# Recurrence of an LSTM layer: the matmul blocks of a step reordered and cut, the output gate apart, and the sums of outputs by accumulating DMAs

## The chip, the cores and the metric

The kernel runs on one core of a Trainium2 chip. The metric is device time in microseconds (us) for the whole kernel, the median of several runs. A second number, the span, comes from one profiled execution: it reaches from the first to the last instruction that the profiler recorded.

The engines are PE (TensorE; PEld is its weight load), DVE (VectorE), ACT (ScalarE), POOL (GpSimd) and SP (SyncE, which here only issues DMAs). SBUF is the on-chip memory of 128 partitions, PSUM the memory that PE writes to.

## The reference

Two layers over x of shape 32 x 512 x 256. The first is graph attention and a Mamba block, the second graph attention and an LSTM. The LSTM runs over the 512 positions of each of the 32 sequences, with hidden size 256, one position after the other. What matters here is this last part (names as in the reference):

```
def step(carry, xp):
    h, c = carry
    gates = xp + h @ W_hh.T
    i, f, g, o = jnp.split(gates, 4, axis=-1)
    c = jax.nn.sigmoid(f) * c + jax.nn.sigmoid(i) * jnp.tanh(g)
    h = jax.nn.sigmoid(o) * jnp.tanh(c)
    return ((h, c), h)
...
logits = jnp.einsum('bth,lh->btl', lstm_out, W_lin) + b_lin
g = jax.lax.stop_gradient(jnp.argmax(logits, axis=-1).astype(lstm_out.dtype))[..., None]
w = g * lstm_out
inc = jnp.cumsum(w, axis=1)
prefix = inc - w
suffix = inc[:, -1:, :] - inc
return 2.0 * lstm_out + prefix * fw_att + suffix * bw_att
```

The result is added to the layer's input x. With two logits, the argmax is a comparison of a difference with a level.

## The kernel before

**Up to 2541 us** the graph and Mamba layers run (`layers_per_batch`). Among this work, POOL also prepares the LSTM's weights in DRAM (`recurrence_weights`): gates in another order, halves folded in, and the rows fw and bw scaled by 0.5. The layers' result lies in DRAM as X3.

**The recurrence** (`recurrence`, one step per t, 512 steps in 32 chunks of CH = 16). The state of 32 sequences times 256 hidden units is laid out on 128 partitions as 4 quarters (Q) of 32 sequences, with J = 64 hidden units each along the free axis. These 64 are two halves of H = 32. Every step does:

- PE multiplies h by the weights `whh`. h is in two tiles, h[0] and h[1], one for each half (called h0 and h1 below). The gate columns of a quarter, 258, are in two PSUM banks: pg0 with 96 columns (the gates f, i, g of half 0, three times 32), and pg1 with 162 (the same gates of half 1, 96; o of both halves, 64; and two columns for the logits). `part` issues four blocks, h0 for pg0, h0 for pg1, h1 for pg0, h1 for pg1, of four matmuls each, one per quarter, side by side in the array. A float32 matmul shows as two records. All of them add to what `x_part` has put in the banks one step ahead: the input's share of the gates, 16 more matmuls for the next step, behind the four blocks in PE's queue.
- ACT takes tanh of pg0 (L1472), then of 160 columns of pg1 (L1473, half 1's gates and o together). A sigmoid is made of a tanh with the halves folded into the weights.
- DVE computes for each half ab (L1478) and the new cell state z (L1481); ACT takes tanh of it (L1483); DVE computes hh (L1491) and transposes it into h0 or h1 (L1495) for the next step.
- DVE then selects by the logits (g, L1502), does one item of the list `extra`, and adds g to the running sum pp (L1508). At the first step of a chunk it also copies the last pp into the new tile (L1510).

PE, DVE and ACT execute in the order in which the code is written (a manual schedule); SP and POOL are ordered by the framework's scheduler, each in its own queue.

`extra` holds the work of the chunk before and after: four `stats` (bn_stats of the next inputs, L1336; the fourth also has POOL compute rstd, L132 and L134), four `norms` taken two per step (L1342; each with a POOL memset), and ten items of `results`. `turning` says at which steps of the chunk PE transposes a normalised input tile: 5, 6, 10, 11.

`results` makes the outputs of the previous chunk on DVE, in two halves of 8 positions: x3 (the residual, loaded by SP from X3 at L1364) plus hh (L1378), plus pp times fw (L1381, L1384), minus pp times bw (L1387, L1390), each on 128 x 512. SP then stores x3 into R, a tile in SBUF that gathers all outputs (L1399).

**The end.** What is still missing is the total times bw. `tot` (L1513) is spread by 16 small DMAs from SP, ACT and POOL into `tots` (L1518); the results of the last chunk are made; then 17 DVE operations add `tots` to R (L1526), and each is followed by four stores to `out`, two on SP and two on ACT (L1528).

Of the kernel before, what the change touches and what calls it, by code (L numbers as in the profile page):

```python
# [9 lines left out]
F32 = mybir.dt.float32  # L10
# [3 lines left out]
AF = mybir.ActivationFunctionType  # L14
ALU = mybir.AluOpType
# [4 lines left out]
P = 128  # L20
N = 512
NT = N // P
D = 256
DK = D // P
# [9 lines left out]
GB = 32  # L34
CH = 16
# [1144 lines left out]
def recurrence_weights(nc, pool, a, wr, now):  # L1180
# [8 lines left out]
    Q, J = 4, 64  # L1189
    W = 4 * J + 2  # L1190
# [3 lines left out]
    order = (3, 1, 0, 2)  # L1194
# [30 lines left out]
    for l in range(2):  # L1225
        for q in range(Q):
            nc.gpsimd.dma_start(
                out=wl[q * 32 : (q + 1) * 32, l * DK : (l + 1) * DK],
                in_=a.wl[q : q + 1, l * J : (l + 1) * J].rearrange("o (k p) -> p (o k)", p=32),
# [12 lines left out]
    t, _ = ordered(b[0], Q, 1, 1.0)  # L1242
# [6 lines left out]
    for n, src in enumerate((a.fw, a.bw)):  # L1249
        for q in range(Q):  # L1250
            nc.gpsimd.dma_start(out=t[q * GB : (q + 1) * GB, n * J : (n + 1) * J], in_=src[q : q + 1, :].to_broadcast([GB, J]))
        yield
    nc.gpsimd.tensor_scalar(t[:, : 2 * J], t[:, : 2 * J], 0.5, None, ALU.mult)
    yield
    nc.gpsimd.dma_start(out=wr[:, n0 : n0 + 2 * J], in_=t[:, : 2 * J])
    yield
# [33 lines left out]
def recurrence(ctx, tc, c, a, X3, wr, out):  # L1290
# [25 lines left out]

    TQ = T // 4
    R = wp.tile([P, TQ, D], F32, name="R")


    NX = CH // 4
# [35 lines left out]

        return tuple([lambda f=f, n=n: f(n) for n in range(NX)] for f in (stats, norm, turn))

    def results(t0, hh, pp):  # L1360

        x3 = ch.tile([P, CH, J], F32, tag="x3", name=f"x3_{t0}")
        for q in range(Q):
            nc.sync.dma_start(  # L1364
                out=x3[q * GB : (q + 1) * GB],
                in_=X3[t0 : t0 + CH, :, q * J : (q + 1) * J].rearrange("t b j -> b t j"),
            )
        todo = []
        n = CH // 2
        for s in (slice(0, n), slice(n, CH)):  # L1370
            r = x3[:, s, :]
            pf = pp[:, s.start : s.stop, :]
            pb = pp[:, s.start + 1 : s.stop + 1, :]
            m = st.tile([P, n, J], F32, tag="m", bufs=1, name=f"m{t0}_{s.start}")
            bc = [P, n, J]

            def one_(r=r, s=s):
                nc.vector.tensor_tensor(r, r, hh[:, s, :], ALU.add)  # L1378

            def two_(m=m, pf=pf):  # L1380
                nc.vector.tensor_tensor(m, pf, fw.unsqueeze(1).to_broadcast(bc), ALU.mult)  # L1381

            def three(r=r, m=m):
                nc.vector.tensor_tensor(r, r, m, ALU.add)  # L1384

            def four(m=m, pb=pb):
                nc.vector.tensor_tensor(m, pb, bw.unsqueeze(1).to_broadcast(bc), ALU.mult)  # L1387

            def five(r=r, m=m):
                nc.vector.tensor_tensor(r, r, m, ALU.subtract)  # L1390

            todo += [one_, two_, three, four, five]
        last_ = todo.pop()

        def gathered():
            last_()
            tq, r0 = t0 // TQ, t0 % TQ
            for q in range(Q):
                nc.sync.dma_start(  # L1399
                    out=R[tq * GB : (tq + 1) * GB, r0 : r0 + CH, q * J : (q + 1) * J], in_=x3[q * GB : (q + 1) * GB]  # L1400
                )

        return todo + [gathered]


    PARTS = ((0, 3 * H), (3 * H, W))

    def part(pg, w, lhs, order, start, stop):

        for k, n in order:  # L1410
            p, (s, e) = pg[n], PARTS[n]
            for q in range(Q):
                nc.tensor.matmul(  # L1413
                    p[q * GB : (q + 1) * GB, :], lhs[k], w[:, k, q, s:e],
                    start=(start and k == 0), stop=(stop and k == DK - 1),
                )

    def x_part(t, xT):

        pg = [psg.tile([P, e - s], F32, tag=f"pg{n}", name=f"pg{n}_{t}") for n, (s, e) in enumerate(PARTS)]  # L1420
        r = (t % G) * GB
        part(pg, wih, [xT[t % CH // G][:, k, r : r + GB] for k in range(DK)], ((0, 0), (1, 0), (0, 1), (1, 1)), True, t == 0)
        return pg

    with tc.manual_schedule(engines={mybir.EngineType.PE, mybir.EngineType.DVE, mybir.EngineType.Activation}):
# [18 lines left out]
        for t in range(T + 1):  # L1444
            s = t % CH
            last = t == T
            if s == 0 and not last:
                t0 = t
                hh_was, pp_was = hh, pp
                hh = ch.tile([P, CH, J], F32, tag="hh", name=f"hh{t0}")  # L1450
                if t:
                    pp = ch.tile([P, CH + 1, J], F32, tag="pp", name=f"pp{t0}")
                assert not extra and not turning
                xT, nxt = nxt, [None] * 2
                stats, norms, turns = normalised(t0 + CH, nxt) if t0 + CH < T else ([], [], [])
                more = results(t0 - CH, hh_was, pp_was) if t else []
                both = [lambda fs=norms[n : n + 2]: [f() for f in fs] for n in range(0, len(norms), 2)]
                extra = stats + both + more
                turning = {(5, 6, 10, 11)[n]: f for n, f in enumerate(turns)}
            if last:  # L1460

                pg = [None, psg.tile([P, W - 3 * H], F32, tag="pg1", name="pglast")]
                part(pg, whh, h, ((0, 1), (1, 1)), True, True)
            elif t:
                part(pg, whh, h, ((0, 0), (0, 1), (1, 0), (1, 1)), False, True)
            pgs = pg
            if not last:
                if t + 1 < T:
                    pg = x_part(t + 1, xT if t + 1 < t0 + CH else nxt)
                turned = [turning.pop(s)()] if s in turning else []  # L1470

                nc.scalar.activation(z[:, H : 4 * H], pgs[0], AF.Tanh)  # L1472
                nc.scalar.activation(z[:, 5 * H : 10 * H], pgs[1][:, : 5 * H], AF.Tanh)  # L1473
                z2 = st.tile([P, 12 * H + 1], F32, tag="z", name=f"z{t + 1}")
                for n in range(2):
                    c0 = 4 * n * H
                    ab = st.tile([P, 2 * H], F32, tag=f"ab{n}", name=f"ab{n}_{t}")
                    nc.vector.scalar_tensor_tensor(  # L1478
                        ab, z[:, c0 + 2 * H : c0 + 4 * H], 1.0, z[:, c0 : c0 + 2 * H], ALU.add, ALU.mult
                    )  # L1480
                    nc.vector.scalar_tensor_tensor(z2[:, c0 : c0 + H], ab[:, :H], 0.5, ab[:, H:], ALU.mult, ALU.add)  # L1481
                for n in range(2):
                    nc.scalar.activation(z[:, (10 + n) * H : (11 + n) * H], z2[:, 4 * n * H : (4 * n + 1) * H], AF.Tanh, scale=0.5)  # L1483

                nc.scalar.copy(z2[:, 12 * H :], level)
                for f in turned:
                    f()
                h = []
                for n in range(2):
                    half = hh[:, s, n * H : (n + 1) * H]  # L1490
                    nc.vector.scalar_tensor_tensor(  # L1491
                        half, z[:, (8 + n) * H : (9 + n) * H], 1.0, z[:, (10 + n) * H : (11 + n) * H], ALU.add, ALU.mult
                    )
                    h.append(st.tile([P, GB], F32, tag=f"h{n}", name=f"h{n}_{t}"))
                    nc.vector.transpose(h[n], half)  # L1495
                z = z2
            if t:

                i = (t - 1) % CH
                p_, h_ = (pp_was, hh_was) if s == 0 and not last else (pp, hh)  # L1500
                g_ = st.tile([P, J], F32, tag="g", name=f"g{t}")
                nc.vector.scalar_tensor_tensor(  # L1502
                    g_, pgs[1][:, 5 * H : 5 * H + 1].to_broadcast([P, J]), level, h_[:, i, :], ALU.is_gt, ALU.mult,
                )
            if extra and not last:
                extra.pop(0)()
            if t:
                nc.vector.tensor_tensor(p_[:, i + 1, :], p_[:, i, :], g_, ALU.add)  # L1508
                if s == 0 and not last:
                    nc.vector.tensor_copy(pp[:, 0, :], p_[:, CH, :])  # L1510
# [1 line left out]
        tot = wp.tile([P, J], F32, name="tot")  # L1512
        nc.vector.tensor_tensor(tot, pp[:, CH, :], bw, ALU.mult)  # L1513

        tots = wp.tile([P, D], F32, name="tots")
        for n in range(4 * Q):
            tq, q = n // Q, n % Q
            (nc.sync, nc.scalar, nc.gpsimd)[n % 3].dma_start(  # L1518
                out=tots[tq * GB : (tq + 1) * GB, q * J : (q + 1) * J], in_=tot[q * GB : (q + 1) * GB]
            )  # L1520
        for f in results(T - CH, hh, pp):
            f()
        t0 = 0
        for step in [2, 6] + [8] * (TQ // 8 - 1):
            r = R[:, t0 : t0 + step, :]
            nc.vector.tensor_tensor(r, r, tots.unsqueeze(1).to_broadcast([P, step, D]), ALU.add)  # L1526
            for tq in range(4):
                (nc.sync, nc.scalar)[tq % 2].dma_start(  # L1528
                    out=out[:, tq * TQ + t0 : tq * TQ + t0 + step, :], in_=r[tq * GB : (tq + 1) * GB]
                )  # L1530
            t0 += step


PERIOD, PIECES = 100234, 49
# [121 lines left out]
```

## Time and profile before

| | us |
|---|---|
| median of 3 runs | 3853.72 (3853.17 to 3853.76) |
| the profiled execution's own time | 3853.91 |
| its span | 3852.2 |

Busy time in the span: PE 3417.8 us (89%), DVE 3256.5 (85%), ACT 2403.0 (62%), POOL 1510.6 (39%). The mean granted TensorE clock is 0.975 of full speed.

How to read the rows. A row of the timeline has the start in us from the span's start, the length, the engine, the line of the kernel, the operation, output<-inputs by the kernel's names, the shapes, the number of instructions merged into the row, and in brackets the idle time of the engine before it with what ended it. A row of the waits has the waiting engine and line, what it waited for, the total in us, the number of times and the longest. A row of the windows has the stretch, its length, busy us and number of instructions of PE, PEld, DVE, ACT and POOL, then the granted clock, the share of the 16 DMA engines and GB/s. A row of the groups has line, engine, operation, shapes and count, then busy us and the mean ns of one, then the idle time before and what ended it. A matmul's end is modelled, and matmuls overlap, so the starts are what is compared.

### The profile page before, as it was taken

The numbers are of one execution on the slowest core, as the hardware profiler recorded it, in microseconds if no ns is written. First come the engines' busy times: TensorE is split into PE (matmuls) and PEld (weight loads), VectorE is DVE, ScalarE is ACT, GpSimd is POOL, SyncE is SP. The second block draws the span as 40 slices with busy tenths as digits, with TensorE's granted clock in tenths as the row PEclk, the third lists the DMA queues.
The fourth block names the chain that finished last, engine by engine and source line by source line (L and its number), as shares of the span: only waits on it lengthen the run. The fifth ranks groups of instructions, "written<-read, shape, count | busy, mean of one in ns | idle before, by whom it ended". The sixth has DMA issues, their size and how long they took to land. (4 is left out here: it accounts for less than half of the span.)

```text
span 3852.2 us, 117182 instructions
## 1 busy us (share of the span) xinstructions
PE 3417.8 (89%) x47370; PEld 2313.5 (60%) x47370; DVE 3256.5 (85%) x10671; ACT 2403.0 (62%) x6434; POOL 1510.6 (39%) x1581
## 2 busy tenths in 40 slices
PE   5999999999999999999999998668888888888882
PEld 3466566556656656655665664446666666666661
DVE  3888888888888888888888886459999999999997
ACT  2777777777777777777777775435454544444441
POOL 3456556555555655655555566710000000000000
PEclk8999999999999999999999998789999999999996
DMA  3322322222223232232223212221222222222226
GB/s 98 89 91 73 101 85 75 94 86 86 83 93 90 72 102 86 72 95 86 86 83 96 87 61 59 82 66 41 44 46 43 46 43 46 43 46 43 46 40 191
DMA packets 271800, 288.76 MB, mean 75 GB/s; under 512 B 151589, under 2 KB 221953, under 8 KB 269073
## 3 DMA queue, kind: packets, MB, share of 16 engines
q1 hardware_dynamic: 265248, 266.96, 25.0%
q10 hardware_dynamic: 3152, 8.76, 0.7%
q8 instruction: 375, 6.14, 0.7%
q0 software_dynamic: 2848, 5.45, 0.5%
q14 instruction: 177, 1.44, 0.1%
HBM read 227.09 MB, written 37.11 MB: 69 GB/s over the span
## 5 line engine op out<-in xcount | busy, mean ns | idle before, releaser
L1413 PE MATMUL pg<-wall,h 128*32 128x96 f32 x16352 | 559.0, 277 | 176.8 <-DVE h L1495 169.4
L1413 PEld LDWEIGHTS pg<-wall,h 128*32 128x32 f32 x16352 | 374.4, 109 | 350.8 <-DVE h L1495 331.9
L1413 PE MATMUL pg<-wall,xTr 128*32 128x96 f32 (+1 forms) x16384 | 549.0, 274 | 0.0
L1413 PEld LDWEIGHTS pg<-wall,xTr 128*32 128x32 f32 x16384 | 447.2, 110 | 5.2 <-issue 0.3
L132 POOL TENSOR_SCALAR ve<-mv 128x4 f32<-128x4 f32 x32 | 6.3, 195 | 1038.5 <-DVE mv L1337 1038.5
L1472 ACT ACTIVATE z<-pg 128x96 f32<-128x96 f32 x512 | 128.7, 251 | 438.9 <-PE pg L1413 438.9
L102 DVE SCALAR_TENSOR_TENSOR w<-rb,colsa,adjT 128x512 f32<-128x512 f32 x512 | 380.4, 778 | 6.0 <-DMA rb<-linea 6.0
L102 DVE SCALAR_TENSOR_TENSOR acc<-px,convw,acc 128x511 f32<-128x511 f32 (+2 forms) x480 | 335.3, 735 | 7.6 <-ACT acc L102 6.4
L1483 ACT ACTIVATE z<-z 128x32 f32<-128x32 f32 x1024 | 234.7, 229 | 168.5 <-DVE z L1481 100.9
L102 ACT ACTIVATE g<-bc,cs 128x128 f32<-128x128 f32 x1024 | 326.0, 399 | 13.1 <-PE py L102 13.1
L102 PE MATMUL px<-mT,win 128*128 128x512 f32 x640 | 307.2, 603 | 0.0
L102 PE MATMUL po<-wc,xh 128*128 128x256 f32 x1024 | 254.3, 392 | 13.5 <-POOL xh L102 8.4
L102 POOL TENSOR_SCALAR ve<-bnmv 128x4 f32<-128x4 f32 x96 | 18.8, 196 | 626.3 <-DVE bnmv L102 607.7
L102 PE MATMUL pav<-w,hb 128*64 128x512 f32 x1024 | 250.1, 608 | 8.0 <-DVE w L102 8.0
L102 PE MATMUL pov<-wb,wv 128*128 128x257 f32 x1024 | 250.5, 392 | 7.0 <-DVE wv L102 5.8
L1495 DVE STREAM_TRANSPOSE h<-hh 128x32 f32<-128x32 f32 x1024 | 216.4, 211 | 34.8
L102 PE MATMUL pz<-mT,win 128*128 128x512 f32 x512 | 245.4, 602 | 0.0
L102 POOL TENSOR_TENSOR rs<-ve,mhalf 128x4 f32<-128x4 f32 (+1 forms) x192 | 237.8, 1239 | 13.3
L1478 DVE SCALAR_TENSOR_TENSOR ab<-z 128x64 f32<-128x64 f32 x1024 | 226.0, 221 | 15.3 <-ACT z L1472 12.0
L102 PEld LDWEIGHTS po<-wc,xh 128*128 128x128 f32 x1024 | 189.5, 193 | 76.6 <-issue 27.0
L1481 DVE SCALAR_TENSOR_TENSOR z<-ab 128x32 f32<-128x32 f32 x1024 | 196.9, 192 | 35.1
L102 POOL TENSOR_SCALAR msk<-adj 128x1024 bf16<-128x1024 int32 x64 | 218.8, 3434 | 13.0 <-DMA adj<-in_adj_dram 7.9
(258 smaller groups left out, 7987.8 us busy)
## 6 DMA issues: line engine op xcount, KB each, us to landing
bc<-line SPq DMA_DIRECT2D x128, 512.0 KB
adj<-in_adj_dram SPq DMA_DIRECT2D x32, 1024.0 KB
rb<-linea SPq DMA_DIRECT2D x64, 512.0 KB
ce<-line SPq DMA_DIRECT2D x64, 384.0 KB
x<-in_x_dram SPq DMA_DIRECT2D x32, 512.0 KB
X<-x SPq DMA_DIRECT2D x32, 512.0 KB
xt<-X SPq DMA_DIRECT2D x128, 128.0 KB
x<-X SPq DMA_DIRECT2D x128, 128.0 KB
```

The source lines that it names most:

```text
L102: return getattr(getattr(self.nc, engine), op)(*map(real, a), **{n: real(v) for n, v in k.items()})
L132: nc.gpsimd.tensor_scalar(ve, var, scale, eps, ALU.mult, ALU.add)
L1413: nc.tensor.matmul(p[q * GB : (q + 1) * GB, :], lhs[k], w[:, k, q, s:e], start=(start and k == 0), stop=(stop and k == DK - 1),)
L1472: nc.scalar.activation(z[:, H : 4 * H], pgs[0], AF.Tanh)
L1478: nc.vector.scalar_tensor_tensor(ab, z[:, c0 + 2 * H : c0 + 4 * H], 1.0, z[:, c0 : c0 + 2 * H], ALU.add, ALU.mult)
L1481: nc.vector.scalar_tensor_tensor(z2[:, c0 : c0 + H], ab[:, :H], 0.5, ab[:, H:], ALU.mult, ALU.add)
L1483: nc.scalar.activation(z[:, (10 + n) * H : (11 + n) * H], z2[:, 4 * n * H : (4 * n + 1) * H], AF.Tanh, scale=0.5)
L1495: nc.vector.transpose(h[n], half)
```

## The change

Four edits.

- The order of the blocks in PE's queue: h0 for pg0; h0 for the columns 0 to 110 of pg1; h1 for pg0; h0 for the columns 110 to 162 of pg1; h1 for pg1.
- ACT's second tanh is split into 96 columns (half 1's gates) and 64 (o).
- The outputs of a chunk are summed by three accumulating DMAs from POOL (hh, pp times fw, pp times bw, added to x3 in SBUF); DVE only makes the products, eight of 128 x 256 in place of ten operations of 128 x 512. bw is negated in the weights for that. The norms are taken one per step, and the order of the extras and the steps of `turning` change: four stats, one product, four norms, seven products; turns at 6, 7, 10, 11.
- At the end, the total is spread over the partitions by four matmuls with a selection matrix `sel` (made by four POOL copies) into PSUM and subtracted from R there; the products of the last chunk come behind the second and third of these operations, and its stores to R are issued by POOL.

```diff
-    nc.gpsimd.tensor_scalar(t[:, : 2 * J], t[:, : 2 * J], 0.5, None, ALU.mult)
+    for n, scale in enumerate((0.5, -0.5)):
+        nc.gpsimd.tensor_scalar(t[:, n * J : (n + 1) * J], t[:, n * J : (n + 1) * J], scale, None, ALU.mult)
...
+        nc.gpsimd.dma_start(out=x3, in_=hh, accum_op=ALU.add)
         todo = []
...
+        for n, w in enumerate((fw, bw)):
+            m = ch.tile([P, CH, J], F32, tag=f"m{n}", bufs=1, name=f"m{n}_{t0}")
+            for s in range(0, CH, 4):
+
+                def product(n=n, w=w, m=m, s=s):
+                    nc.vector.tensor_tensor(
+                        m[:, s : s + 4, :], pp[:, s + n : s + n + 4, :], w.unsqueeze(1).to_broadcast([P, 4, J]), ALU.mult
+                    )
+                    if s + 4 == CH:
+                        nc.gpsimd.dma_start(out=x3, in_=m, accum_op=ALU.add)
+
+                todo.append(product)
...
+    CUT = 110
+    WHOLE = tuple((k, n, 0, W) for n in range(2) for k in range(DK))
+    LATER = ((0, 0, 0, W), (0, 1, 0, CUT), (1, 0, 0, W), (0, 1, CUT, W), (1, 1, 0, W))
...
-                part(pg, whh, h, ((0, 0), (0, 1), (1, 0), (1, 1)), False, True)
+                part(pg, whh, h, LATER, False, True)
...
-                both = [lambda fs=norms[n : n + 2]: [f() for f in fs] for n in range(0, len(norms), 2)]
-                extra = stats + both + more
-                turning = {(5, 6, 10, 11)[n]: f for n, f in enumerate(turns)}
+                extra = stats + more[:1] + norms + more[1:] if t else stats + norms
+                turning = {(6, 7, 10, 11)[n]: f for n, f in enumerate(turns)}
...
-                nc.scalar.activation(z[:, H : 4 * H], pgs[0], AF.Tanh)
-                nc.scalar.activation(z[:, 5 * H : 10 * H], pgs[1][:, : 5 * H], AF.Tanh)
+                for n in range(2):
+                    nc.scalar.activation(z[:, (4 * n + 1) * H : (4 * n + 4) * H], pgs[n][:, : 3 * H], AF.Tanh)
+                nc.scalar.activation(z[:, 8 * H : 10 * H], pgs[1][:, 3 * H : 5 * H], AF.Tanh)
...
+            if T // 2 <= t < T // 2 + Q:
+                q = t - T // 2
+                nc.gpsimd.tensor_copy(
+                    sel[:, q, :].rearrange("p (t b) -> p t b", b=GB),
+                    c.ident[:, q * GB : (q + 1) * GB].unsqueeze(1).to_broadcast([P, 4, GB]),
+                )
...
-        for f in results(T - CH, hh, pp):
-            f()
+        tots = psx.tile([P, DK, P], F32, tag="px", name="tots").rearrange("p k e -> p (k e)")
+        for q in range(Q):
+            nc.tensor.matmul(
+                tots[:, q * J : (q + 1) * J],
+                sel[:, q, :], tot,
+                start=True, stop=True,
+            )
+        rest = results(T - CH, hh, pp, nc.gpsimd)
...
-            nc.vector.tensor_tensor(r, r, tots.unsqueeze(1).to_broadcast([P, step, D]), ALU.add)
+            nc.vector.tensor_tensor(r, r, tots.unsqueeze(1).to_broadcast([P, step, D]), ALU.subtract)
...
+            if n:
+                for f in rest[:4]:
+                    f()
+                rest = rest[4:]
```

More of the change, by code (lines that the diff above doesn't have):

```diff
@@ L1318, in recurrence @@
     R = wp.tile([P, TQ, D], F32, name="R")
+    sel = wp.tile([P, Q, P], F32, name="sel")
     NX = CH // 4
@@ L1358, in normalised, with results @@
         return tuple([lambda f=f, n=n: f(n) for n in range(NX)] for f in (stats, norm, turn))
-    def results(t0, hh, pp):
+    def results(t0, hh, pp, queue=nc.sync):
         x3 = ch.tile([P, CH, J], F32, tag="x3", name=f"x3_{t0}")
@@ L1367, in results @@
             )
+        nc.gpsimd.dma_start(out=x3, in_=hh, accum_op=ALU.add)
         todo = []
[L1369 to L1392, printed above, removed]
+        for n, w in enumerate((fw, bw)):
[8 more added lines that the diff above has]
+                todo.append(product)
         last_ = todo.pop()
@@ L1398, in gathered @@
             for q in range(Q):
-                nc.sync.dma_start(
+                queue.dma_start(
                     out=R[tq * GB : (tq + 1) * GB, r0 : r0 + CH, q * J : (q + 1) * J], in_=x3[q * GB : (q + 1) * GB]
@@ L1406, in recurrence @@
     PARTS = ((0, 3 * H), (3 * H, W))
+    CUT = 110
+    WHOLE = tuple((k, n, 0, W) for n in range(2) for k in range(DK))
+    LATER = ((0, 0, 0, W), (0, 1, 0, CUT), (1, 0, 0, W), (0, 1, CUT, W), (1, 1, 0, W))
     def part(pg, w, lhs, order, start, stop):
-        for k, n in order:
+        for k, n, c0, c1 in order:
             p, (s, e) = pg[n], PARTS[n]
+            s, e = s + c0, min(s + c1, e)
             for q in range(Q):
                 nc.tensor.matmul(
-                    p[q * GB : (q + 1) * GB, :], lhs[k], w[:, k, q, s:e],
+                    p[q * GB : (q + 1) * GB, s - PARTS[n][0] : e - PARTS[n][0]], lhs[k], w[:, k, q, s:e],
                     start=(start and k == 0), stop=(stop and k == DK - 1),
@@ L1421, in x_part @@
         r = (t % G) * GB
-        part(pg, wih, [xT[t % CH // G][:, k, r : r + GB] for k in range(DK)], ((0, 0), (1, 0), (0, 1), (1, 1)), True, t == 0)
+        part(pg, wih, [xT[t % CH // G][:, k, r : r + GB] for k in range(DK)], WHOLE, True, t == 0)
         return pg
@@ L1456, in recurrence @@
                 more = results(t0 - CH, hh_was, pp_was) if t else []
-                both = [lambda fs=norms[n : n + 2]: [f() for f in fs] for n in range(0, len(norms), 2)]
-                extra = stats + both + more
-                turning = {(5, 6, 10, 11)[n]: f for n, f in enumerate(turns)}
+                extra = stats + more[:1] + norms + more[1:] if t else stats + norms
+                turning = {(6, 7, 10, 11)[n]: f for n, f in enumerate(turns)}
             if last:
                 pg = [None, psg.tile([P, W - 3 * H], F32, tag="pg1", name="pglast")]
-                part(pg, whh, h, ((0, 1), (1, 1)), True, True)
+                part(pg, whh, h, WHOLE[DK:], True, True)
             elif t:
-                part(pg, whh, h, ((0, 0), (0, 1), (1, 0), (1, 1)), False, True)
+                part(pg, whh, h, LATER, False, True)
             pgs = pg
@@ L1513, in recurrence @@
         nc.vector.tensor_tensor(tot, pp[:, CH, :], bw, ALU.mult)
[L1515 to L1519, printed above, removed]
-            )
-        for f in results(T - CH, hh, pp):
-            f()
+        tots = psx.tile([P, DK, P], F32, tag="px", name="tots").rearrange("p k e -> p (k e)")
[4 more added lines that the diff above has]
+                start=True, stop=True,
+            )
+        rest = results(T - CH, hh, pp, nc.gpsimd)
         t0 = 0
-        for step in [2, 6] + [8] * (TQ // 8 - 1):
+        for n, step in enumerate([2, 6] + [8] * (TQ // 8 - 1)):
+            assert not rest or t0 + step <= TQ - CH
             r = R[:, t0 : t0 + step, :]
-            nc.vector.tensor_tensor(r, r, tots.unsqueeze(1).to_broadcast([P, step, D]), ALU.add)
+            nc.vector.tensor_tensor(r, r, tots.unsqueeze(1).to_broadcast([P, step, D]), ALU.subtract)
             for tq in range(4):
```

## The prediction

> **What bounds the kernel now.** I read the page first (span, share by engine, chain), then the waits between 2620 and 3776 us, then the timeline of one step of the recurrence, then the windows of the end.
>
> The span is 3852.2 us. Up to 2541 us the graph and Mamba layers run; on PE, DVE and ACT the change leaves their instructions and order there as they are. From 2553 to 3785 us the 512 steps of the recurrence run. From there to 3852 us the outputs leave.
>
> ```profile
> span 3852.2 us, 117182 instructions
> ...
> DVE 27%; PE 3%; issue 2%; DMA 1%; ACT 1%; SPq 0%; DVEq 0%
> ```
>
> ```profile
> ACT z L1472 <- PE pg L1413: 410.9, 480, 1.0
> PEld pg L1413 <- DVE h L1495: 312.8, 480, 1.0
> ```
>
> The chain puts most on DVE, but it steps back to whatever came just before on the engine. The waits say otherwise: in each of the 480 steps of that window ACT waits for PE and PE waits for DVE's transpose, so the step is a ring of dependences. The timeline of one step shows it (PE's rows are answers for windows of some hundredths of a us, so each begins with the oldest matmul in flight there):
>
> ```profile
> 2992.01 0.21 DVE L1495 STREAM_TRANSPOSE h<-hh 128x32 f32<-128x32 f32 x1
> 2992.37 0.21 DVE L1495 STREAM_TRANSPOSE h<-hh 128x32 f32<-128x32 f32 x1
> ...
> 2992.67 0.68 DVE L1378 TENSOR_TENSOR x<-x,hh 128x512 f32<-128x512 f32 x1
> 2993.27 0.22 DVE L1508 TENSOR_TENSOR pp<-pp,g 128x64 f32<-128x64 f32 x1
> 2993.44 0.22 DVE L1478 SCALAR_TENSOR_TENSOR ab<-z 128x64 f32<-128x64 f32 x1
> 2993.70 0.19 DVE L1481 SCALAR_TENSOR_TENSOR z<-ab 128x32 f32<-128x32 f32 x1
> 2993.81 0.22 DVE L1478 SCALAR_TENSOR_TENSOR ab<-z 128x64 f32<-128x64 f32 x1
> ...
> 2994.18 0.19 DVE L1491 SCALAR_TENSOR_TENSOR hh<-z 128x32 f32<-128x32 f32 x1
> 2994.41 0.21 DVE L1495 STREAM_TRANSPOSE h<-hh 128x32 f32<-128x32 f32 x1
> ```
>
> ```profile
> 2993.16 0.25 ACT L1472 ACTIVATE z<-pg 128x96 f32<-128x96 f32 x1 [0.53 <-PE pg L1413]
> 2993.43 0.30 ACT L1473 ACTIVATE z<-pg 128x160 f32<-128x160 f32 x1
> ```
>
> ```profile
> 2992.64 0.13 PEld L1413 LDWEIGHTS pg<-wall,h 128*32 128x32 f32 x4
> ```
>
> ```profile
> 2992.74 0.49 PE L1413 MATMUL pg<-wall,h 128*32 128x96 f32 x12
> ```
>
> The ring of h0, in ns from these records: transpose end to PE's first weights 53, to the first tanh 882, to ab 283, to z 258, to the next tanh 227, to hh 261, to the transpose 225, the transpose 211: 2400. The transposes are 2.400 us apart in nearly every step, whatever DVE's extra work; the exception is the first step of a chunk (2.508), where bn_stats and the copy at L1510 make DVE late.
>
> The last two rows show what can go. The weights of h1 are loaded at 2992.637, but its matmuls begin only at 2992.740, because PE still streams h0's block for bank pg1. A pass is four matmuls side by side; each block is two passes. Passes of 96 columns start 82.5 ns apart, of 162 columns 137.5, which is 2.5 ns + 0.833 ns a column; the transposes' 128 columns fit too (110).
>
> **The order of the matmuls.** In ns from the first weights: streaming begins at 26; now h1's block for pg0 begins at 26 + 2x82.5 + 2x137.5 = 466, and the tanh 416 later (882). After, h0's block for pg1 stops at 110 columns (94 a pass), so PE is free at 26 + 165 + 188 = 379, and h1's weights, at 363, need the same 26: 389. The tanh starts at 805: 77 ns less per step. PE's passes rise from 16 to 18 a step, in its idle time.
>
> Then h0's other 52 columns (46 a pass by the law) and h1's block for pg1: its second pass begins at 389 + 165 + 92 + 137.5 = 783 instead of 768. ACT's second tanh followed that by 389 ns: at 1172 instead of 1157.
>
> **o apart.** That tanh shrinks from 160 to 96 columns: 252 ns by the row at L1472 instead of 304. It ends at 1424, and ab for half 1 can start 31 later, at 1455. DVE is free for it 368 ns after the first ab (2993.807 - 2993.439), at 805 + 283 + 368 = 1456. So h1 stays 363 ns behind h0 and nothing is given back. In one piece it would end at 1476, ab would be 51 late, and, as hh of half 0 stands behind z of half 1 on DVE with 15 ns to spare, most of the gain would go. The added o tanh (64 columns) goes through ACT between the second tanh and the next: 64 columns from PSUM freed ACT after 121 ns or less in the first phase, and the next tanh needs ACT at 1573. Cover enough.
>
> **DVE's extras.** With a ring of 2323, the first ab must start 1353 ns after the transpose begins (211 + 53 + 805 + 283). Today's extra of 512 columns (next start 599 ns later) lets it start at 1397 (362 to the second transpose, 136 to g, 160 to the extra, 599, 140 for pp): 44 of the 77 would be lost, 33 left. The change leaves eight products of 256 columns per chunk, one per step; the additions go to DMAs. Their spacing is not in the trace; bounds: half of 599, and 599. By the durations of 128x512 (681) and 128x64 (212) a column costs 1.04 ns, so 66 of the 599 are fixed and 256 columns take 333: ab can start at 1131. With bn_stats it is about 1348: just enough. The norms, one instead of two per step, take about 330. The 30 chunk starts stay at 2.508.
>
> So 512 steps, less the first (no h yet), less 30, and the end: 480 x 0.077 = 37.0 us. The turns now at steps 6, 7, 10, 11 end on PE some 0.2 us ahead of the next h; they move by 15 ns against 77: I price them at nothing, at most 124 x 0.03 = 4 us.
>
> **The accumulating DMAs.** Three per chunk on POOL, 93 beside the steps. POOL takes 0.60 us to issue one (below). They wait for x3, hh, m and each other; behind them on POOL stand the rstd of the next chunk (four steps after) and the memsets; on SP, the stores to R wait for the last sum, and behind these the loads of xt, which have until the next chunk. An accumulating DMA isn't in the trace: nearest rows, 2.2 us for 128 KB (the chain's "DMA x<-X", L1364) and 2.4 us to landing for 258 KB at L1286. The first sum of products is issued about at step 11, the second at 15, and the rstd is needed at step 4 or 5 of the next chunk: the first may take about 9 steps, 21 us, before anyone waits. Price nothing.
>
> **The start.** Four POOL copies for sel and one more POOL operation for the weights lie in POOL's idle time (17.7 us before L132 at 2543.75). Nothing.
>
> **The end.** The windows and the busy rows from 3785 us on:
>
> ```profile
> 3785.00:3795.00 10.00, 0.76 (x16) 0.35 (x16) 9.39 (x20) 0.19 (x2) 2.57 (x5) 0.60 0.07 14
> ...
> 3805.00:3829.00 24.00, 0.00 (x0) 0.00 (x0) 24.00 (x11) 0.00 (x0) 0.00 (x0) 0.50 1.01 337
> ```
>
> ```profile
> L1518 POOL DMA_DIRECT2D tots<-tot x5 | 2.6, 522 | 63.5 <-DVE tot L1513 63.4
> ...
> L1387 DVE TENSOR_TENSOR m<-pp,wall 128x512 f32<-128x512 f32 x2 | 1.4, 692 | 0.1
> ```
>
> DVE's ten operations on results keep the first R add until 3793.84; SP's first store waits until 3797.7, behind tots and R. After, tot goes through four matmuls (about 1.4 us by the cold transposes, 0.69 a pair), and R starts near 3788.5, 5.3 earlier. Two groups of four products (1.33 each) come between the first adds, so from the fourth add on DVE is 2.7 ahead. But the DMA engines are full (1.01; a block of 1 MB takes 3.1 us in both queues). They gain those 2 to 3 us and SP's 3 us, and must carry two more accumulations of 512 KB (1.5 each as a plain copy, 3 if read and write count). I take 2.5 less, bounds 6 less and 3 more. The last R adds need the sums at about 3822, and they should land near 3815.
>
> **Sum.** 37.0 + 2.5 = 39.5 off the profiled execution's 3853.91 gives 3814.4; the median is 0.2 lower: **3814 us**. What a measurement of this kernel can tell from no change is 0.2%, 7.7 us.
>
> **Rivals.** (A) The short passes cost more than their columns. Bounds: 46 ns, and 82.5 as for 96 columns. At 82.5 the second tanh comes 73 ns later; DVE's ab and the hh queued behind it are late by as much, and 5 ns of 77 are left: 2.4 us plus the end, 3849. At 64, midway, 40 ns are left: 3833. Against it: weights and matmul of four tiles follow each other every 6.6 ns at a step's start, so eight instructions take 26. [...]
>
> (B) The products cost 599 ns a step, by waits or slower DVE: half the 480 steps gain 33 instead of 77, 480 x 0.055 = 26, and 2.5: 3825.
>
> (C) Slower: POOL's issuing blocks DVE. 93 issues at 0.60 us are 56 us if each stops DVE for its whole time; 3853.7 + 56 - 39.5 = 3870. It decides from 0.50 us an issue ((39.5 + 7.7) / 93). Against it: at the end POOL issues five while DVE runs products, and their duration (692) is that of the later ones with POOL idle (684 to 692). [...] The row decides.
>
> (D) Accumulations of over 21 us hold POOL's rstd and so the norms: 31 x (landing - 21); at 22.3 the gain is gone. Nearest rows are a tenth of that.
>
> **Chances.** Forecast 0.77 (own range 3806 to 3823), A 0.09, B 0.06, C 0.05, D 0.03. The low end is 87 ns a step (h1's weights ready 10 ns sooner: 42 us) and 6 at the end: 3806. The high end takes in B and A's middle: 3836. Faster is the forecast, B and 0.05 of A: 0.88; same is 0.03 of A, near its end; slower is C, D and the last 0.01 of A: 0.09.
>
> **What would show it.** Transposes 2.32 us apart; h1's first matmul about 25 ns after its weights; the first tanh 805 ns after h0's weights; ab for half 1 still about 368 after that for half 0; 2.51 at chunk starts; the first R add some 2.4 us after pglast's last matmul ends (3786.1; now 7.7); DVE rows no longer while POOL issues. Wrong if the period is above 2.36, or if DVE is idle before ab for half 1.

## The result, and the profile after

The changed kernel takes 3860.02 us (median of 20 runs, 3845.54 to 3873.69), the kernel before beside it 3853.46 (20 runs, 3850.59 to 3856.61). The ratio is 1.0021, 95% interval 1.0012 to 1.0030: 0.2% slower, where 1% faster was forecast. The runs of the new kernel also spread nearly five times as far.

From the page of the kernel after (groups: busy time, mean ns | idle time before them, and what ended it; then a DMA queue, and the median time from issue to landing):

```profile
span 3859.3 us, 126092 instructions
...
q0 software_dynamic: 16704, 56.27, 7.5%
...
L1408 PE MATMUL pg<-wall,xTr 128*32 128x96 f32 (+1 forms) x16384 | 568.6, 274 | 24.0 <-issue 23.0
L1408 PEld LDWEIGHTS pg<-wall,xTr 128*32 128x32 f32 x16384 | 448.0, 110 | 48.0 <-issue 30.3
...
x<-m POOLq DMA_DIRECT2D x64, 512.0 KB, 6.5
```

The same groups and queue on the page of before, with the row of q8, the queue that brings instructions:

```profile
q8 instruction: 375, 6.14, 0.7%
q0 software_dynamic: 2848, 5.45, 0.5%
...
L1413 PE MATMUL pg<-wall,xTr 128*32 128x96 f32 (+1 forms) x16384 | 549.0, 274 | 0.0
L1413 PEld LDWEIGHTS pg<-wall,xTr 128*32 128x32 f32 x16384 | 447.2, 110 | 5.2 <-issue 0.3
```

Before, the two PE groups had 0.0 and 5.2 us of idle time in front of them. After, the matmuls of `x_part` have 23.0 us of idle time ended by "issue": PE waited for nothing that the profile shows. The waits of the recurrence, 2620 to 3776 us (total, times, longest), say the same:

```profile
ACT z L1467 <- PE pg L1408: 401.1, 493, 3.4
...
PEld pg L1408 <- DVE h L1490: 248.7, 447, 0.9
...
PEld pg L1408 <- issue: 43.4, 48, 2.3
PE pg L1408 <- issue: 32.5, 38, 2.0
```

The ring is there as before (ACT for PE, PE for the transpose), but two rows are new. PE and PEld overlap, so the two are not to be added.

An ordinary step is what the prediction wanted. The timeline around 2992 us (start, duration):

```profile
2991.04 0.22 DVE L1473 SCALAR_TENSOR_TENSOR ab<-z 128x64 f32<-128x64 f32 x1 [0.15 <-ACT z L1467]
...
2991.40 0.22 DVE L1473 SCALAR_TENSOR_TENSOR ab<-z 128x64 f32<-128x64 f32 x1
...
2992.01 0.21 DVE L1490 STREAM_TRANSPOSE h<-hh 128x32 f32<-128x32 f32 x1
```

The next ab starts at 2993.36, 2.32 after the last, and DVE waits 0.15 us for ACT before it, where its extra used to stand in the way. A bad step, the one from 2698.69 us on, looks like this on PE, DVE and ACT:

```profile
2697.72 0.62 PE L1408 MATMUL pg<-wall,xTr 128*32 128x96 f32 x15
2700.22 0.60 PE L1408 MATMUL pg<-wall,xTr 128*32 128x162 f32 x9 [1.89 <-issue]
```

```profile
2698.69 0.21 DVE L1490 STREAM_TRANSPOSE h<-hh 128x32 f32<-128x32 f32 x1
```

```profile
2701.38 0.62 ACT L1467 ACTIVATE z<-pg 128x96 f32<-128x96 f32 x2 [2.50 <-PE pg L1408]
```

h0 is ready at 2698.90, yet PE does nothing until 2700.22, and then first does the rest of `x_part`, matmuls whose inputs had long been there. It looks as if PE had no instructions, and the DMA queues support that. These are their answers for 2692.1 to 2697.7 us and then for 2697.7 to 2701 us (packets, MB, share of 16 engines):

```profile
DMA packets 815, 0.79 MB, mean 140 GB/s; under 512 B 559, under 2 KB 687, under 8 KB 815
...
q0 software_dynamic: 143, 0.52, 50.1%
q1 hardware_dynamic: 672, 0.26, 17.4%
```

```profile
q8 instruction: 1, 0.02, 1.8%
q14 instruction: 1, 0.01, 0.6%
```

The first covers 5.6 us in which queue q8, which brings 16 KB of instructions with each packet, brought none. The accumulating DMA x<-m on q0 fills these engines (their busy share is 0.98 from 2694.7 to 2697.2); single records show its 128 packets of 4096 B, about 340 ns each, which is eight for each of the 16 engines, from 2694.57 to 2697.80. The refill of q8 starts at 2697.80, as they end. It takes 0.95 us, and PE runs again 1.5 us after that. The refill before it had come at 2691.04.

Over the recurrence q8 brings 291 such packets (259 before), 12% more, as PE has 12% more matmul records there (37022 for 32933), one every 4.00 us in the median (4.74 before). After, 38 intervals are longer than 5.5 us, up to 6.84. Of the 39 steps that are over 0.3 us late, 33 have such an interval beside them and two more follow such a step; the other four, 0.34 to 0.40 us late, have none. The records also hint at what a late refill waits for: a transfer's 128 records are followed by 16 of 4 bytes, as many as there are engines, and 27 of the 38 late refills start within 0.03 us of such a record, as if they had waited for an engine to end its share of the transfer. Steps over 2.65 us are late by 36.9 us in all. The balance of the profiled execution, from the first transpose of h0 to its last and on to the end: 480 steps times 71 ns are 34.1 us won, 36.9 us lost in long steps and some 2 us in smaller ones, so the loop went from 1232.3 to 1237.4; the end from 67.2 to 71.9.

### The profile page after: what moved, and what is told of

Same layout as the page of the kernel before. It is cut to its first block, busy times and chain, and to the rows that moved or that the text cites. A ratio compares the mean times of both kernels' runs of the same rounds, so it can differ in the third digit from the quotient of the medians.

```text
span 3859.3 us, 126092 instructions
## 1 busy us (share of the span) xinstructions
PE 3443.3 (89%) x51466; PEld 2325.5 (60%) x51466; DVE 3169.9 (82%) x10607; ACT 2430.8 (63%) x6946; POOL 1591.6 (41%) x1681
## 5 line engine op out<-in xcount | busy, mean ns | idle before, releaser
L1408 PE MATMUL pg<-wall,h 128*32 128x96 f32 x20440 | 577.7, 255 | 135.9 <-DVE h L1490 124.3
L1408 PE MATMUL pg<-wall,xTr 128*32 128x96 f32 (+1 forms) x16384 | 568.6, 274 | 24.0 <-issue 23.0
L1408 PEld LDWEIGHTS pg<-wall,h 128*32 128x32 f32 x20440 | 389.1, 109 | 304.6 <-DVE h L1490 266.6
L1467 ACT ACTIVATE z<-pg 128x96 f32<-128x96 f32 x1024 | 256.3, 250 | 487.0 <-PE pg L1408 429.4
L102 DVE BATCH_NORM_STATS2 bnst<-x 128x6 f32<-128x256 f32 x384 | 145.7, 414 | 92.5 <-POOL x L102 88.9
```

What stands on the lines that cost most here:

```text
L102: return getattr(getattr(self.nc, engine), op)(*map(real, a), **{n: real(v) for n, v in k.items()})
L1408: nc.tensor.matmul(p[q * GB : (q + 1) * GB, s - PARTS[n][0] : e - PARTS[n][0]], lhs[k], w[:, k, q, s:e], start=(start and k == 0), stop=(s ...
L1467: nc.scalar.activation(z[:, (4 * n + 1) * H : (4 * n + 4) * H], pgs[n][:, : 3 * H], AF.Tanh)
```

## The experiments

**Theory F (fetch)**: PE's instruction refills wait behind the data of an accumulating transfer, and PE runs dry. **Rival I (issue)**: POOL's issuing of these DMAs (0.92 us each in the kernel after) holds DVE, as rival (C) of the prediction had it. **Rival P (program)**: the new order has 36 matmuls a step for 32, and such a program can't be brought in fast enough, with or without these transfers. "Loop" is from the first transpose of h0 to its last, "end" from there to the end of the span, "long steps" the time by which steps over 2.65 us exceed the median step; all are worked out from the trace of the profiled run.

| kernel | us | ratio to before (95%) | loop | end | refills >5.5 us apart | long steps |
|---|---|---|---|---|---|---|
| before | 3853.46 | 1 | 1232.3 | 67.2 | 17 | 1.2 |
| after | 3860.02 | 1.0021 (1.0012-1.0030) | 1237.4 | 71.9 | 38 | 36.9 |
| order_only | 3836.86 | 0.9943 (0.9929-0.9957) | 1209.4 | 66.8 | 0 | 0.3 |
| sums_only | 3864.01 | 1.0016 (1.0007-1.0025) | 1235.6 | 70.7 | 47 | 4.3 |
| quarters | 3831.84 | 0.9931 (0.9917-0.9944) | 1203.4 | 71.9 | 0 | 4.7 |
| pool_adds | 3970.40 | 1.0293 (1.0279-1.0307) | 1346.1 | 65.3 | 39 | 104.8 |
| halves | 3838.94 | 0.9956 (0.9942-0.9969) | 1212.0 | 68.2 | 3 | 12.3 |
| plain_copies | 3825.30 | 0.9919 (0.9905-0.9932) | 1201.7 | 64.9 | 3 | 2.4 |
| plain_twice | 3867.50 | 1.0027 (1.0017-1.0038) | 1245.0 | 73.2 | 21 | 45.9 |
| spread | 3830.16 | 0.9928 (0.9914-0.9942) | 1206.4 | 67.6 | 1 | 6.0 |
| late_tail | 3826.71 | 0.9927 (0.9913-0.9941) | 1206.5 | 62.4 | 1 | 5.6 |

The kernel before had medians of 3855.9 to 3857.4 beside the experiments. The mark of 5.5 us serves for counting; it is not the point at which PE runs dry, as `before` and halves show. The profiled run of plain_twice was the slowest of its eight (3876.7 us).

**order_only**: the order of the matmuls and o apart, and nothing else of the change.

```
-    part(pg, whh, h, ((0, 0), (0, 1), (1, 0), (1, 1)), False, True)
+    part(pg, whh, h, LATER, False, True)
-    nc.scalar.activation(z[:, H : 4 * H], pgs[0], AF.Tanh)
-    nc.scalar.activation(z[:, 5 * H : 10 * H], pgs[1][:, : 5 * H], AF.Tanh)
+    for n in range(2):
+        nc.scalar.activation(z[:, (4 * n + 1) * H : (4 * n + 4) * H], pgs[n][:, : 3 * H], AF.Tanh)
+    nc.scalar.activation(z[:, 8 * H : 10 * H], pgs[1][:, 3 * H : 5 * H], AF.Tanh)
```

> Kernel before with the new order of the recurrent products and o apart alone; the sums stay on VectorE in 512 columns and no accumulating transfer is issued. Theory F (fetch): TensorE's instruction refills (16 KB each on queue 8, one every 4.0 us in the kernel after) are held up behind the 512 KB accumulating transfers, and TensorE runs out of instructions; without them no refill comes more than 5.5 us after the one before, no step is over 2.65 us, the period is 2.32 to 2.33 us in most steps, and the time is 3853 - 36 = 3817, up to 3830 where the 512-column sums take some of it. Rival P (program): the added matmuls (36 for 32 in a step) alone make the refills too frequent; stalls of 0.5 to 3 us stay, 20 us or more of them, and the time is 3840 to 3850. Rival I (issue): GpSimd's writing of the transfers' descriptors holds VectorE; here it says the same as F.

Measured: 0.57% faster. Of PE's recurrent matmuls and their weights, only this row in the waits (same window) has no releaser:

```profile
PEld pg L1417 <- issue: 0.9, 4, 0.3
```

No refill comes later than 5.47 us after the one before, though there are as many as in the kernel after. P falls. The gain, 20.5 us against its own before of 3857.4, is less than the 23 to 36 that F gave, and 3836.9 us lies above F's range, because of DVE's extras of 512 columns: the period is 2.355 in their steps, 2.40 in the two with two norms, and 2.33 in those with bn_stats. ab starts 325 ns after the first tanh there instead of 282.

**sums_only**: the other part alone, the sums by transfers and the new end with the old order.

```
-    LATER = ((0, 0, 0, W), (0, 1, 0, CUT), (1, 0, 0, W), (0, 1, CUT, W), (1, 1, 0, W))
+    LATER = ((0, 0, 0, W), (0, 1, 0, W), (1, 0, 0, W), (1, 1, 0, W))
```

(and the two tanh as before.)

> Kernel after with the old order of the recurrent products and the old two gate activations; the accumulating transfers and the new end stay. F: TensorE uses up 16 KB of instructions in 4.7 us instead of 4.0, so that the same waits of about 3 us behind a transfer leave little or no stall: period 2.40 as before, stalls (steps over 2.65) worth 0 to 12 us, and the end 5 us longer: 3854 to 3868. I: the same stalls as in the kernel after, about 41 us, on top of the old period: 3890 to 3900. P: no stalls, 3856 to 3859.

Measured: 0.16% slower. The refills come late (47 intervals over 5.5 us, up to 7.17; 17 in the kernel before, up to 6.25), but only nine steps are long, by 4.3 us, and the row in the waits is small:

```profile
PEld pg L1408 <- issue: 4.3, 9, 1.0
```

That fits a PE which uses up 16 KB in 4.73 us and so holds out longer when a refill is late. Rival I gave the same stalls again; it falls. So neither part alone stalls PE for more than 4.3 us: it takes the transfers and the quicker use of instructions together.

**quarters**: the same bytes in four times as many transfers.

```
-        nc.gpsimd.dma_start(out=x3, in_=hh, accum_op=ALU.add)
+        def quarter(s, src):
+            nc.gpsimd.dma_start(out=x3[:, s : s + 4, :], in_=src[:, s : s + 4, :], accum_op=ALU.add)
...
-                    if s + 4 == CH:
-                        nc.gpsimd.dma_start(out=x3, in_=m, accum_op=ALU.add)
+                    if n == 0:
+                        quarter(s, hh)
+                    quarter(s, m)
```

> Kernel after with each accumulating transfer of 512 KB cut into four of 128 KB (four steps of time each), issued with the product that completes them: twelve issues in a chunk instead of three, the same bytes. F: a refill waits behind at most one or two pieces (0.7 to 1.4 us instead of 3), so no interval over 5.5 us and no stall over 0.3 us; time 3815 to 3826. I: four times as many issues by GpSimd, so stalls of 40 us or more, up to 160: 3860 to 3980. P: as after, 3860.

Measured: 0.69% faster, with four times the issues. 3831.8 us lies 6 above F's range, and nine steps are over 0.3 us late where F allowed none. The waits:

```profile
PEld pg L1411 <- issue: 8.6, 22, 0.8
...
PE pg L1411 <- issue: 2.4, 10, 0.4
```

A piece takes 128 packets of 1024 B at 112 ns, 0.9 us of the engines instead of 2.7. POOL's issues take 0.88 us each here and 0.92 in the kernel after (medians; the prediction had 0.60), and in the latter DVE's instructions that run beside one last as long as the others (ab 224 ns with and without, z 192, the products 417). I is out. Two steps per chunk keep a residue: pieces of hh bunch in POOL's queue before steps 14 and 0 (some of its 4.7 us), and step 0 takes 2.414 us in the median instead of 2.329. Why step 0 does was not tried apart; in spread, where pieces of hh go out at other steps, it takes 2.331.

**pool_adds**: additions by POOL in the place of the transfers.

```
-            nc.gpsimd.dma_start(out=x3[:, s : s + 4, :], in_=src[:, s : s + 4, :], accum_op=ALU.add)
+            r = x3[:, s : s + 4, :]
+            nc.gpsimd.tensor_tensor(r, r, src[:, s : s + 4, :], ALU.add)
```

(against quarters.)

> Kernel after with the sums made by GpSimd additions of 256 columns (twelve in a chunk) in place of the accumulating transfers; the end too. F: no long transfer, no stall over 0.3 us; the period is 2.32 to 2.33 if GpSimd's additions do not slow VectorE, time 3808 to 3820 (the end is shorter too, with no accumulating transfers beside the stores). I: no descriptors are written for sums, so the same. P: stalls as after, some 40 us: 3850 to 3860. If GpSimd's additions hold VectorE for their own duration (estimate 0.6 to 0.7 us each from the 512-column row of 1.27 us), 31 x 12 x up to 0.65 = up to 240 us more.

Measured: 2.9% slower, by the last mechanism of that list:

```profile
2999.29 0.73 POOL L1372 TENSOR_TENSOR x<-x,m 128x256 f32<-128x256 f32 x1 [2.20 <-DVE m L1380]
```

```profile
2999.49 0.62 DVE L1477 SCALAR_TENSOR_TENSOR ab<-z 128x64 f32<-128x64 f32 x1
3000.14 0.19 DVE L1480 SCALAR_TENSOR_TENSOR z<-ab 128x32 f32<-128x32 f32 x1
3000.25 0.22 DVE L1477 SCALAR_TENSOR_TENSOR ab<-z 128x64 f32<-128x64 f32 x1
```

The first ab starts beside the addition, takes 0.62 us and ends at 3000.11, 0.09 after the addition; the second starts when POOL is idle again and takes 0.22. In the kernel after, ab takes 224 ns beside POOL's issuing of a DMA as without it. So here an addition by POOL held DVE's ab, and an issue didn't; by what means is not shown. The 39 late refills here stand in much longer steps and say nothing on F.

**halves**: two transfers of 256 KB for each of 512.

```
-                    if s + 4 == CH:
-                        nc.gpsimd.dma_start(out=x3, in_=m, accum_op=ALU.add)
+                    if s % 8 == 4:
+                        nc.gpsimd.dma_start(out=x3[:, s - 4 : s + 4, :], in_=m[:, s - 4 : s + 4, :], accum_op=ALU.add)
```

(hh likewise.)

> Kernel after with each 512 KB accumulating transfer cut into two of 256 KB. F (refills wait behind a whole transfer): a refill is held up 1.3 to 1.6 us instead of 2.7 to 3.1 by one transfer, more where two follow each other; intervals between refills reach 5 to 5.9 us, few stalls, worth 2 to 15 us: time 3832 to 3845, between quarters (3832) and after (3860). I (GpSimd's issues hold VectorE): refuted by quarters already; would give more stall than after.

Measured: 12.3 us of long steps, between 36.9 for whole transfers and 4.7 for quarters; 3838.9 us, inside F's range. The packets of 2048 B take 188 ns, eight of them 1.5 us. Only three refills come over 5.5 us apart; beside most of the 22 long steps the interval is 4.4 to 5.5 us.

**plain_copies** and **plain_twice**: is it the adding, or the time?

```
-        nc.gpsimd.dma_start(out=x3, in_=hh, accum_op=ALU.add)
+        nc.gpsimd.dma_start(out=x3, in_=hh)
+        nc.gpsimd.dma_start(out=x4, in_=hh)      # plain_twice only
```

(m likewise.)

> Kernel after with the three transfers of a chunk as plain copies of the same 512 KB from the same queue, which overwrite instead of adding (the sums are left out). If the length of the transfer counts (F): a 4096 B packet took 340 ns when it accumulated; if a plain one takes half, the hold-up is about 1.4 us and nearly all stalls go, time 3822 to 3835 (the end is shorter too); if it takes as long, stalls stay near 40 us and the time near 3860. Rival G (the queue or its descriptors, not the time the data take): stalls as after at any packet time, about 3855.

> Kernel plain_copies with every plain copy of 512 KB made twice, the second into a tile that nothing reads (the sums are left out). One copy kept the 16 engines for 1.5 us, two in a row keep them for 3.0, as long as one accumulating transfer. F: what counts is how long a refill stands behind data, so the stalls come back, 20 to 45 us of them, intervals between refills up to 6.5 us, time 3843 to 3866. Rival A (it is the adding that disturbs, not the time taken): stalls stay at 2 to 6 us; with the longer end the time is 3826 to 3834.

Measured: a plain packet of 4096 B takes 162 ns, half of an adding one's. Single copies leave 2.4 us of long steps (3825.3 us, inside F's range; G is out), doubled ones 45.9. The issue rows of plain_copies and then of plain_twice:

```profile
PEld pg L1408 <- issue: 9.3, 20, 1.1
...
PE pg L1408 <- issue: 3.9, 10, 0.8
```

```profile
PEld pg L1411 <- issue: 44.7, 45, 2.5
PE pg L1411 <- issue: 34.2, 32, 2.3
```

Nothing adds in plain_twice, and the stall is back (its 3867.5 us lie 1.5 above the range given). The size is not to be set beside the 36.9 of the kernel after: 26 of the 45.9 us lie in eight steps in which PE's clock also fell (see the last section) and the eight behind them, against 5.7 of 36.9 in the kernel after. The other 20 us are still eight times what single copies leave. What counts in these runs is how long the engines are filled without a break, not what the transfer does. What a refill waits for shows in part: eight records for each engine, 8 x 341 ns, are 2.7 us; where two transfers of 512 KB followed each other (2625.26 to 2632.08 us in the kernel after), a refill started at 2628.51, with the last 4-byte record of the first transfer, and did not wait for the second. Of the 67 refills of that run that start while a transfer runs, 39 start in the last fifth of its time and three between 40% and 80%. That a refill waits until an engine has ended its share of the one transfer is the author's reading of this; how it goes with the two copies in a row that bring the stall back in plain_twice is not shown.

**spread** and **late_tail**: a version from these results. Pieces of hh are issued at steps 7 and 8 of their chunk and 0 and 2 of the next (the first of them four steps after it is complete), x3 has three buffers, and the last chunk's sums return to VectorE; late_tail then makes them one product at a time behind the fourth and later adds on R.

```
+                if s in (7, 8):
+                    quarter(x3, 4 * (s - 7), hh)
+                if t >= CH and s in (0, 2):
+                    quarter(x3_was, 8 + 2 * s, hh_was)
...
-            if n:
-                for f in rest[:4]:
+            if n > 3:              # late_tail only
+                for f in rest[:1]:
```

> Kernel quarters with the pieces of hh issued as soon as their four steps are done, so that fewer pieces queue up together, x3 with three buffers, and in the last chunk the remaining sums made by VectorE between the additions on R instead of by transfers. F: no refill later than 5.5 us after the one before, steps 14 and 0 lose their residue: loop 1196 to 1203 us (quarters 1203.4). The end, which is bound by the 16 DMA engines, loses the 2.1 MB of the last four accumulating transfers: 62 to 66 us from the last transpose instead of 71.9. Time 3816 to 3827. If the end is not bound by those transfers, it stays at 70 to 72 and the time at 3828 to 3832.

> Kernel spread with the last chunk's sums one product at a time behind the fourth and later additions on R, instead of four at a time behind the second and third, where VectorE left the stores' queues empty. If the end is bound by the stores' packets (55 us of 16 engines, the first issued 4.5 us after the last transpose), it takes 61 to 64 us instead of 67.6, and the time is 3823 to 3827; if not, 66 to 68 and 3828 to 3832. The loop as in spread, 1201 to 1208.

Measured: spread misses. Its loop is 1206.4 us, no better than quarters, and its 3830.2 us lie above the range given. Steps 14 and 0 lost most of their residue (means 2.341 and 2.346), but steps 9 to 12, where a piece comes in nearly every step, grew (2.365 to 2.376), and one refill came 5.7 us after the one before where none over 5.5 was expected. Its end took 67.6 us: the sums on DVE, four products at a time, put 5.5 and 5.4 us between the second, third and fourth add on R, and the stores ran out of work (from 3771.9 us the DMA queues moved 0 GB/s for 1.7 us). late_tail's took 62.4, as expected of an end that the DMA engines bound (transfers are 53.7 us of it, worked out below); its loop is the same. With 3826.7 us, 29 less than before beside it, it is the fastest of the kernels with all sums, though its ratio doesn't differ from those of spread and quarters by more than their intervals.

## Why the prediction was wrong

**The ring: right.** In the median step of the kernel after, in ns: transpose end to weights 53, to the first tanh 808 (805 forecast, 882 before), to ab 282, ab of half 1 another 369 later (368); h1 stays 367 behind h0 (363). The second tanh follows the first by 367, so the short passes cost by their columns and rival (A) is out. The period is 2.329 where 2.323 was forecast: 71 of the 77 ns.

**DVE's extras: right in kind.** Products of 256 columns hide (2.33 in their steps); (B) is out. Against 512 columns they are worth less than the 44 ns a step that the prediction gave: order_only shows 26.

**"The accumulating DMAs ... Price nothing": this step failed.** The prediction asked who waits for the landing of the sums: POOL, SP, the loads. Nobody does, as it said; 6.5 us to landing is well under the 21 of rival (D). It didn't ask who else uses the 16 engines. PE's instructions do, and the page of before showed it (q8, 375 packets, 6.14 MB). Each 512 KB sum takes 2.7 us of every engine (8 x 341 ns), twice the time of a copy (8 x 162); a refill behind it came up to 6.84 us after the one before, and a PE that uses up 16 KB in 4.0 us ran dry. In the profiled execution the term was 37 us, not 0 (5.7 of them in the steps where the clock fell too).

**"PE's passes rise ..., in its idle time": right for PE, wrong for its supply.** The array has the time (between 2620 and 3776 us it still waits 115.9 us for DVE's transpose, 159.9 before), but PE uses up 16 KB of instructions in 4.0 us instead of 4.7. sums_only shows what that is worth: the same transfers cost 4.3 us with the old order.

**(C): its size was near, its mechanism wrong.** It gave 3870 from POOL's issues. Loss per transfer, 36.9 / 93 = 0.40 us, is of that order, but quarters has four times the issues and an eighth of the loss.

**The end: wrong sign.** 2.5 us less was forecast (6 less to 3 more); 4.7 more was measured. The first add did start earlier, 4.1 us after the last transpose of h0 instead of 8.8, 4.8 of the 5.3 forecast. But here are the DMA queues of the end, 67 us before and 72 us after:

```profile
q1 hardware_dynamic: 4032, 8.96, 42.5%
q10 hardware_dynamic: 1872, 8.43, 38.2%
```

```profile
q10 hardware_dynamic: 1632, 8.39, 37.9%
q1 hardware_dynamic: 1632, 8.39, 35.8%
q0 software_dynamic: 624, 2.10, 16.4%
```

The shares times the window are 54.1 us of 16 engines before and 64.9 after. Three sums were added, at 2.7 us or more each (q0's 11.8 us less the 3.1 that late_tail has there without sums leave 8.7); the prediction counted two, at 1.5 to 3. About 10.8 us more of transfers against 4.8 less of waiting leave 6.0, and 4.7 was measured. In late_tail, the queues of the last 63 us, without the sums:

```profile
q10 hardware_dynamic: 1632, 8.39, 41.4%
q1 hardware_dynamic: 1632, 8.39, 39.0%
q0 software_dynamic: 192, 0.52, 4.9%
```

These are 53.7 us, and with the early start the end is 62.4. So the forecast of the end had the right idea about what bounds it, and the wrong price for what was put there.

**The signs it named for the loop** came out: the period, the first tanh, ab of half 1, the chunk starts, DVE's rows beside POOL's issues. They all look at the ordinary step; none looks for steps that stall.

What stays open: late_tail still has 5.6 us of long steps, and the first steps of a chunk are at 2.51. Why runs of the kernel after differ by up to 28 us was not tried; that the place of a refill against a transfer shifts from run to run would explain it, and is only argued.

## What to carry to other kernels

Here a transfer that nobody waited for still took the DMA engines (2.7 us of each for 512 KB that are added), and PE's own instructions came through them (16 KB every 4.0 us). Before moving work to large DMAs beside a PE with many small matmuls, read the instruction queue's row: the interval between refills, how much the change shortens it, and how long one transfer fills the engines. Cut the transfers so that a piece is short against the interval (here 0.9 us against 4.0), and in a stretch that the engines already bound, price every added byte at its own packet time (here 341 ns for 4096 B that are added, 162 for 4096 B that are copied).

## What the hardware did that was not expected

PE's clock fell during two of the stalls. Windows of one us from 2979 (PE, PEld, DVE, ACT, POOL, then the granted clock, DMA share, GB/s):

```profile
2979.00:2980.00 1.00, 0.04 (x1) 0.00 (x0) 0.90 (x7) 0.82 (x5) 0.00 (x0) 1.00 1.01 193
2980.00:2981.00 1.00, 0.59 (x15) 0.59 (x19) 0.93 (x6) 0.04 (x1) 0.00 (x0) 0.73 0.10 16
2981.00:2982.00 1.00, 1.00 (x24) 0.83 (x20) 0.26 (x2) 0.00 (x0) 0.00 (x0) 0.50 0.09 20
2982.00:2983.00 1.00, 1.00 (x33) 1.00 (x29) 0.00 (x0) 0.00 (x0) 0.00 (x0) 0.50 0.00 0
```

From 2980.46 the clock is 0.5 for 3.41 us, and weights take 0.177 us instead of 0.110; this step lasted 5.11 us. PE had been idle for 1.36 us. The other fall followed 1.39 us, while idle times of 1.96, 1.89 and 1.63 us in the same run were followed by none, so the length alone doesn't decide; what does is not shown. The second fall lasted 3.41 us too. In plain_twice it happened eight times, in pool_adds eleven times. In each of the three runs the falls lie whole multiples of 3.413 us apart (182 in the kernel after; 12, 12, 68, 12, 79, 12 and 80 in plain_twice); where that time comes from is not shown either.
